# A two-layer graph network on one core: own rows multiplied in their own round, and a finish in four parts

## The chip, the cores and the metric

The kernel runs on one core of a Trainium2 chip. A core has TensorE (matrix products, written PE in a profile, with its weight loads as PEld), VectorE (DVE), ScalarE (ACT), GpSimd (POOL) and SyncE (SP), each working through its own list of instructions, and sixteen DMA engines. The metric is the device time of one execution in microseconds. The kernel before takes 2129.82 us, the median of three runs (2129.74 to 2130.59).

## The reference

Two layers of message passing over 6250 nodes with 512 features, each followed by a residual sum and a layer normalisation. There are 106,250 edges: 50,000 drawn pairs in both directions and one loop for each node, sorted by destination.

```
def _layernorm(x, axis=-1, eps=1e-05):
    m = jnp.mean(x, axis=axis, keepdims=True)
    v = jnp.var(x, axis=axis, keepdims=True)
    return (x - m) / jnp.sqrt(v + eps)
...
    # layer 0: mean over the edges that end in a node
    x_l = x @ W_l.T + b_l
    agg = jax.ops.segment_sum(x_l[src], dst, num_segments=N_NODES)
    deg = jax.ops.segment_sum(jnp.ones_like(src, dtype=x.dtype), dst, num_segments=N_NODES)
    out_l = agg / jnp.maximum(deg, 1.0)[:, None]
    return out_l + x @ W_r.T
...
    # layer 1: mean over the edges that start in a node
    msg = h[dst] @ W_neigh.T + b_neigh
    neigh = jax.ops.segment_sum(msg, src, num_segments=n)
    neigh = neigh / deg[:, None]
    out = jax.nn.relu(h @ W_self.T + b_self + neigh)
    x = h + out
    return (x - mean) * jax.lax.rsqrt(var + LN_EPS) * ln_gamma + ln_beta
...
    x = _layernorm(x + layer0(x), axis=-1)
    x = _layernorm(x + layer1(x), axis=-1)
```

Everything is float32. A mean of products is the product of a mean, so the kernel averages the neighbour rows first and multiplies the average by the weight.

## The kernel before

**Groups, windows, tiles.** `grouped` (L585) does one layer. The sorted edges are cut into four equal columns, and in each of Q rounds the kernel treats one group: up to four windows (one in each column) of 32 nodes, 128 nodes in all. Layer 0 has 60 groups, layer 1 has 66. The last groups have three windows only, because the fourth column ends earlier: 58 and 59 in layer 0, 63 to 65 in layer 1. A tile is 128 edges of each column. A group owns three or four tiles in layer 0 and three in layer 1.

**One round.** The loop at L778 runs over the groups and issues, by hand, the order in which every engine works; nothing reorders it later. In round g:

- `fetch(g + 1)` (L613) lets GpSimd gather the neighbour rows of the next group, one indirect DMA for each tile and window, 128 rows of 2 KB (L609). There are ten buffers `rows` of four windows each.
- `match(g + 1)` (L627) builds 0/1 matrices `hot` on VectorE, `shrink(g + 1)` (L635) sums them for counting.
- `visits(g, ...)` (L691) are the products of `hot` with the rows into `agg`, one visit for each tile, beginning with the last tile of the group before. Four windows of a visit work side by side in TensorE. The visits are issued in three parts: the first two, the third, the rest.
- `count(g)` (L704) multiplies for the numbers of neighbours; VectorE makes the reciprocal from them. `average(g)` (L723) adds the loops in layer 1 (VectorE, L727) and scales `agg` to `mean` (ScalarE, L731).
- `turn(g, v)` (L733, through `transposed`, L571) turns `mean` or the group's own rows `own` by four transposes into the one PSUM buffer `tp`, which ScalarE copies to `meanT` or `ownT`.
- `dense(g, v)` (L737, through `project`, L579) multiplies by a 512 x 512 weight in four products into `po`; `own` starts the sum, `mean` ends it. `po` has one buffer in layer 0 and two in layer 1.
- `close(g)` (L744) starts the generator `finish0` (L530) or `finish1` (L542): bias, residual, statistics (`spread`, L511, with a square root on ScalarE). `store(g)` (L749) runs its rest two rounds after the visits: normalisation, in layer 1 the scale, the shift, the second residual and the second normalisation with a second square root, and then the write to memory, by SP, or, for the three groups named in `ends` (L593), by a scatter of GpSimd.
- `begin(g + 1)` (L675) loads the own rows of the next group, by SP. For two groups near the end of layer 0 (56 and 57) GpSimd gathers them instead (L683), behind the gathers of the same group's neighbours.

So in the round of group g TensorE does: two visits of g; the mean of g-1 turned; the own rows of g-1 multiplied; the third visit; the mean of g-1 multiplied; the own rows of g turned; the remaining visits; the count. In layer 0, steps of sorting the edges for layer 1 are mixed in at the end of each round (`more`, L768) until the sort is done. Layer 1 gathers from `h_d`, which layer 0 writes, so it starts when the last group of layer 0 is stored.

The part of the loop that sets the order around the change:

```
785                    visits(g, slice(0, 2))
786                if g:
787                    turn(g - 1, "mean")
788                    dense(g - 1, "own")
789                if g > 1:
790                    store(g - 2)
...
798                    turn(g, "own")
```

Of the kernel before, what the change touches and what calls it, by code (L numbers as in the profile page):

```python
# [9 lines left out]
F32 = mybir.dt.float32  # L10
# [3 lines left out]
ALU = mybir.AluOpType  # L14
# [4 lines left out]
P = 128  # L19
# [79 lines left out]
def kernel(  # L99
# [16 lines left out]
    nc = tc.nc  # L116
    N, D = x.shape
# [53 lines left out]
    def both(o, a, b, op):  # L171

        nc.vector.scalar_tensor_tensor(o, a, 1.0, b, op0=ALU.mult, op1=op)  # L173
# [347 lines left out]
    def normalize(y, v, mv, root, nr):  # L521

        nc.vector.reciprocal(root[:nr], root[:nr])
        nc.vector.tensor_scalar(y, v, mv[:nr, 0:1], root[:nr], op0=ALU.subtract, op1=ALU.mult)  # L524

    biases = {}

    def finish0(nr, po, own, some, work):  # L530
        po = po[:nr]
        nc.vector.scalar_tensor_tensor(po, biases["bl"][:nr], some[:nr], po,
                                       op0=ALU.mult, op1=ALU.add)
        v = work.tile([P, D], F32, name="v", bufs=1)
        both(v[:nr], po, own[:nr], ALU.add)
        mv, root = spread(v[:nr], nr, work)
        yield
        y = work.tile([P, D], F32, name="y")
        normalize(y[:nr], v[:nr], mv, root, nr)
        yield y  # L540

    def finish1(nr, po, own, some, work):  # L542
        po = po[:nr]
        if some is None:
            both(po, po, biases["bs + bn"][:nr], ALU.add)
        else:
            nc.vector.scalar_tensor_tensor(po, biases["bn"][:nr], some[:nr], po,
                                           op0=ALU.mult, op1=ALU.add)
            both(po, po, biases["bs"][:nr], ALU.add)
        nc.vector.scalar_tensor_tensor(po, po, 0.0, own[:nr], op0=ALU.max, op1=ALU.add)  # L550
        mv, root = spread(po, nr, work)
        yield
        normalize(po, po, mv, root, nr)
        both(po, po, biases["ga"][:nr], ALU.mult)
        both(po, po, biases["be"][:nr], ALU.add)
        y = work.tile([P, D], F32, name="y")
        both(y[:nr], po, own[:nr], ALU.add)
        mv, root = spread(y[:nr], nr, work)
        normalize(y[:nr], y[:nr], mv, root, nr)
        yield y  # L560
# [24 lines left out]
    def grouped(s, table, w_n, w_s, layer, finish, dest, other):  # L585


        with tc.tile_pool(name=f"g{layer}", bufs=2) as work, tc.tile_pool(
# [152 lines left out]
                project(st["po"], st[v + "T"], w_s if v == "own" else w_n, st["nr"],  # L741
                        v == "own", v == "mean")

            def close(g):  # L744
                st = state[g]
                st["finish"] = finish(st["nr"], st["po"], st["own"], st["some"], work)
                next(st["finish"])

            def store(g):  # L749
# [28 lines left out]
            for g in range(Q + 1):  # L778


                if g + 1 < Q:
                    fetch(g + 1)
                    match(g + 1)
                if g < Q:
                    visits(g, slice(0, 2))
                if g:
                    turn(g - 1, "mean")
                    dense(g - 1, "own")
                if g > 1:
                    store(g - 2)  # L790
                if g + 1 < Q:
                    begin(g + 1)
                if g < Q:
                    visits(g, slice(2, 3))
                if g:
                    dense(g - 1, "mean")
                if g < Q:
                    turn(g, "own")
                    visits(g, slice(3, None))
                    count(g)  # L800
                    average(g)
                if g:
                    close(g - 1)
                more(1, True)
                if g + 1 < Q:
                    shrink(g + 1)
                more(5, False)
# [152 lines left out]
```

## Time and profile before

| What | us |
|---|---|
| median of three runs (2129.74 to 2130.59) | 2129.82 |
| the profiled execution | 2130.99 |
| its span, first to last instruction | 2129.2 |
| first gather of layer 0 starts | 30.38 |
| last gather of layer 0 starts | 1086.68 |
| last store of layer 0 is issued | 1106.62 |
| first gather of layer 1 starts | 1111.16 |
| last gather of layer 1 starts | 2095.39 |
| last store of layer 1 is issued | 2123.92 |

The mean granted clock of TensorE in that execution was 0.984 of full speed.

How to read what follows. A line of a group of instructions gives the source line, the engine, the operation, what it writes and reads (with sizes), how many there were, and behind the bar the busy time in microseconds, the mean duration of one in nanoseconds, and the idle time of the engine just before them with what ended it. A line of a timeline gives the start and the duration in microseconds, the engine, the source line and the operation, and in brackets how long the engine was idle before it and what it waited for. One product in float32 is two records, so a multiplication by a weight is "x8" and a visit of three windows is "x6". Records of TensorE overlap a little, so the time of a step is best taken from one start to the next.

### The profile page before, as it was taken

The page shows a single profiled execution, that of the slowest core. Times are in us where ns is not written, and L with a number is a line of the kernel's source. Part 1 is how long each engine was busy: PE and PEld are TensorE (multiplying, and loading weights), DVE is VectorE, ACT ScalarE, POOL GpSimd, SP SyncE. Part 2 cuts the span into 40 slices and gives each one's busy share as a digit, 9 for nine tenths or more (in the row PEclk, how much of TensorE's full clock was granted, in tenths as well). Part 3 has the DMA queues.
Part 4 walks back from the last instruction along what each step waited for, and adds up shares of the span by engine and source line. Part 5 has one row for each costly group of instructions (what it writes and reads, how often), then busy time and mean ns, then how long its engine had stood idle before and what let it go on. Part 6 is the DMA issues. An engine that isn't in the chain of part 4 may idle for free.

```text
span 2129.2 us, 26081 instructions
## 1 busy us (share of the span) xinstructions
PE 1945.1 (91%) x7723; PEld 671.4 (32%) x7723; DVE 1185.0 (56%) x2495; ACT 314.6 (15%) x661; POOL 1554.9 (73%) x1638
## 2 busy tenths in 40 slices
PE   4699999999999998999879999999999999999996
PEld 1132333332323333433222333333333333333332
DVE  2574455564555564342433666666666666666576
ACT  0011111111111111111111111111111111111111
POOL 3777777777777777777747777777777777777773
PEclk9899999999999999999989999999999999999998
DMA  7787877878887878888757888888888888888883
GB/s 225 224 242 235 238 237 237 240 238 240 238 239 237 239 236 240 246 237 242 223 151 227 243 246 246 245 246 244 246 242 249 240 249 241 247 242 246 241 247 109
DMA packets 184527, 499.36 MB, mean 235 GB/s; under 512 B 43946, under 2 KB 46436, under 8 KB 184366
## 3 DMA queue, kind: packets, MB, share of 16 engines
q0 software_dynamic: 130128, 426.11, 67.8%
q1 hardware_dynamic: 51406, 65.89, 9.7%
q10 hardware_dynamic: 2832, 5.51, 0.7%
q8 instruction: 66, 1.08, 0.2%
q14 instruction: 95, 0.78, 0.1%
HBM read 464.74 MB, written 32.96 MB: 234 GB/s over the span
## 4 chain that ended last, share of the span: by engine, by line
DMA 32%; POOL 28%; PE 22%; issue 14%; DVE 3%; POOLq 0%; ACT 0%; SPq 0%; DVEq 0%; ACTq 0%
POOL rows L609 28%; DMA rows<-h_d,idx 17%; DMA rows<-in_x_dram,idx 14%; PE po L582 10%; PE agg L700 9%; PE tp L574 2%; DMA val_i<-in_dst_dram 0%; DVE stats L514 0%; PE turn L465 0%; DVE po L173 0%; DMA own<-in_x_dram,slots 0%; PE deg L709 0%; PE turn L438 0%; PE turn L294 0%; DVE agg L727 0%
## 5 line engine op out<-in xcount | busy, mean ns | idle before, releaser
L700 PE MATMUL agg<-rows,hot 128*32 128x512 f32 x4220 | 900.3, 612 | 134.0 <-DMA rows<-in_x_dram,idx 46.1
L609 POOL DMA_INDIRECT rows<-in_x_dram,idx x834 | 800.7, 960 | 266.4 <-issue 224.7
L609 POOL DMA_INDIRECT rows<-h_d,idx x785 | 744.9, 949 | 242.6 <-issue 200.3
L582 PE MATMUL po<-wa,meanT 128*128 128x512 f32 (+1 forms) x1008 | 466.0, 605 | 0.0
L582 PE MATMUL po<-wb,ownT 128*128 128x512 f32 (+1 forms) x1008 | 456.3, 596 | 0.1
L700 PEld LDWEIGHTS agg<-rows,hot 128*32 128x32 f32 x4220 | 157.0, 109 | 655.0 <-DMA rows<-in_x_dram,idx 242.0
L565 DVE TENSOR_SCALAR inv<-deg 128x1 f32<-128x1 f32 (+1 forms) x60 | 9.5, 158 | 490.4 <-PE deg L709 490.4
L582 PEld LDWEIGHTS po<-wa,meanT 128*128 128x128 f32 (+1 forms) x1008 | 180.2, 188 | 286.7 <-issue 256.5
L582 PEld LDWEIGHTS po<-wb,ownT 128*128 128x128 f32 (+1 forms) x1008 | 181.8, 190 | 183.6 <-issue 183.4
L576 ACT COPY ownT<-tp 128x512 f32<-128x512 f32 (+1 forms) x126 | 73.3, 582 | 800.6 <-PE tp L574 800.6
L718 DVE TENSOR_SCALAR loops<-deg 128x1 f32<-128x1 f32 (+1 forms) x66 | 10.4, 158 | 310.9 <-PE deg L709 302.4
L173 DVE SCALAR_TENSOR_TENSOR srt<-srt 128x448 f32<-128x448 f32 (+3 forms) x313 | 180.4, 617 | 4.0
L731 ACT ACTIVATE mean<-agg,inv 128x512 f32<-128x512 f32 (+1 forms) x126 | 86.6, 687 | 359.3 <-DVE some L568 147.2
L640 DVE TENSOR_REDUCE hotb<-hot 128x128 bf16<-128x512 f32 (+1 forms) x126 | 133.8, 1062 | 0.1
L518 ACT ACTIVATE rstd<-mv,eps 128x1 f32<-128x1 f32 (+1 forms) x192 | 56.5, 294 | 438.9 <-DVE mv L516 435.6
L576 ACT COPY meanT<-tp 128x512 f32<-128x512 f32 (+1 forms) x126 | 73.1, 580 | 193.0 <-PE tp L574 192.9
L173 DVE SCALAR_TENSOR_TENSOR hot<-rel,cols 128x640 f32<-128x640 f32 x126 | 98.1, 778 | 0.2 <-DVE bs L173 0.2
L574 PEld LDWEIGHTS tp<-ident,mean 128*128 128x128 f32 (+1 forms) x504 | 52.8, 141 | 110.7 <-issue 43.5
L574 PE MATMUL tp<-ident,mean 128*128 128x128 f32 (+1 forms) x504 | 82.8, 287 | 4.8 <-ACT mean L731 4.8
L574 PEld LDWEIGHTS tp<-ident,own 128*128 128x128 f32 (+1 forms) x504 | 62.7, 141 | 72.8 <-issue 69.7
L574 PE MATMUL tp<-ident,own 128*128 128x128 f32 (+1 forms) x504 | 75.7, 273 | 5.4 <-DMA own<-in_x_dram,slots 5.4
L524 DVE TENSOR_SCALAR po<-po,mv,rstd 128x512 f32<-128x512 f32 (+1 forms) x66 | 54.0, 818 | 2.4
(151 smaller groups left out, 900.1 us busy)
## 6 DMA issues: line engine op xcount, KB each, us to landing
own<-h_d SPq DMA_DIRECT2D x261, 64.0 KB
out_dram<-y SPq DMA_DIRECT2D x250, 64.0 KB
own<-in_x_dram SPq DMA_DIRECT2D x230, 64.0 KB
h_d<-y SPq DMA_DIRECT2D x227, 64.0 KB
rows<-in_x_dram,idx POOLq DMA_INDIRECT x834
rows<-h_d,idx POOLq DMA_INDIRECT x785
wa<-in_L_gnn_W_l_dram ACTq DMA_DIRECT2D x1, 1024.0 KB
wb<-in_L_gnn_W_r_dram ACTq DMA_DIRECT2D x1, 1024.0 KB
```

Of the source, the lines that this page charges most:

```text
L173: nc.vector.scalar_tensor_tensor(o, a, 1.0, b, op0=ALU.mult, op1=op)
L518: nc.scalar.activation(root[:nr], mv[:nr, 1:2], AF.Sqrt, bias=eps[:nr])
L524: nc.vector.tensor_scalar(y, v, mv[:nr, 0:1], root[:nr], op0=ALU.subtract, op1=ALU.mult)
L565: nc.vector.tensor_scalar(inv[:nr], deg, 1.0, None, op0=ALU.max)
L574: nc.tensor.transpose(p[:, k, :nr], v[:nr, k * P:(k + 1) * P], ident[:nr, :nr])
L576: nc.scalar.copy(t[:, :, :nr], p[:, :, :nr])
L582: nc.tensor.matmul(po[:nr], aT[:, k, :nr], w[:, k, :], start=first and k == 0, stop=end and k == NK - 1)
L609: nc.gpsimd.indirect_dma_start(out=t, out_offset=None, in_=table, in_offset=bass.IndirectOffsetOnAxis(ap=s.idx[:, m:m + 1], axis=0))
L640: nc.vector.tensor_reduce(hb[:, 0, :], hots[g][:, s.X * C:n * C].rearrange("p (v c) h -> p (c h) v", c=C), axis=mybir.AxisListType.X, op=A ...
L700: nc.tensor.matmul(agg[H * c:H * (c + 1), :], hot[:, C * (s.X + v) + c, :], chunks[t][c], start=t == ts[0], stop=t == ts[-1])
L718: nc.vector.tensor_scalar(st["loops"][:nr], deg[:nr, 1:2], 1.0, None, op0=ALU.add)
L731: nc.scalar.mul(st["mean"][:nr], st["agg"][:nr], st["inv"][:nr])
```

## The change

The order of a round becomes: two visits of g; `store(g - 2)` and `begin(g + 1)`; the mean of g-1 turned; the third visit; the own rows of g turned; the mean of g-1 multiplied; the remaining visits; the count; the own rows of g multiplied. In the last round of a layer the own rows of g are turned right behind the mean of g-1, and the third visit and the own product stand between the mean product and the last visit.

The finish is cut into four parts. `ready` (end of the group's own round) does what needs only the own rows: in layer 0 bias times share plus own rows into `v`, in layer 1 own rows plus shift into a new tile `add`. `follow` is called twice in the next round: behind the mean product, for the sums with `po` (and the ReLU), and behind `average`, for the statistics. `store` does the rest. In layer 1 the normalisation, scale, shift and second residual, four operations on VectorE, become two: `(po - mean) * scale` and `that * reciprocal root + add`.

```
     def finish0(nr, po, own, some, work):
-        po = po[:nr]
-        nc.vector.scalar_tensor_tensor(po, biases["bl"][:nr], some[:nr], po,
+        v = work.tile([P, D], F32, name="v")
+        nc.vector.scalar_tensor_tensor(v[:nr], biases["bl"][:nr], some[:nr], own[:nr],
                                        op0=ALU.mult, op1=ALU.add)
-        v = work.tile([P, D], F32, name="v", bufs=1)
-        both(v[:nr], po, own[:nr], ALU.add)
+        yield
+        both(v[:nr], po[:nr], v[:nr], ALU.add)
+        yield
         mv, root = spread(v[:nr], nr, work)
...
     def finish1(nr, po, own, some, work):
         po = po[:nr]
+        add = work.tile([P, D], F32, name="add")
+        both(add[:nr], own[:nr], biases["be"][:nr], ALU.add)
+        yield
...
         nc.vector.scalar_tensor_tensor(po, po, 0.0, own[:nr], op0=ALU.max, op1=ALU.add)
+        yield
         mv, root = spread(po, nr, work)
         yield
-        normalize(po, po, mv, root, nr)
-        both(po, po, biases["ga"][:nr], ALU.mult)
-        both(po, po, biases["be"][:nr], ALU.add)
+        nc.vector.reciprocal(root[:nr], root[:nr])
+        nc.vector.scalar_tensor_tensor(po, po, mv[:nr, 0:1], biases["ga"][:nr],
+                                       op0=ALU.subtract, op1=ALU.mult)
         y = work.tile([P, D], F32, name="y")
-        both(y[:nr], po, own[:nr], ALU.add)
+        nc.vector.scalar_tensor_tensor(y[:nr], po, root[:nr], add[:nr],
+                                       op0=ALU.mult, op1=ALU.add)
         mv, root = spread(y[:nr], nr, work)
...
-            def close(g):
+            def ready(g):
                 st = state[g]
                 st["finish"] = finish(st["nr"], st["po"], st["own"], st["some"], work)
+                next(st["finish"])
+
+            def follow(g):
+                st = state[g]
                 next(st["finish"])
...
                 if g < Q:
                     visits(g, slice(0, 2))
-                if g:
-                    turn(g - 1, "mean")
-                    dense(g - 1, "own")
                 if g > 1:
                     store(g - 2)
                 if g + 1 < Q:
                     begin(g + 1)
+                end = g == Q - 1
+                if g:
+                    turn(g - 1, "mean")
+                if g < Q and not end:
+                    visits(g, slice(2, 3))
                 if g < Q:
-                    visits(g, slice(2, 3))
+                    turn(g, "own")
                 if g:
                     dense(g - 1, "mean")
+                    follow(g - 1)
+                if end:
+                    visits(g, slice(2, 3))
+                    dense(g, "own")
                 if g < Q:
-                    turn(g, "own")
                     visits(g, slice(3, None))
                     count(g)
                     average(g)
                 if g:
-                    close(g - 1)
+                    follow(g - 1)
+                if g < Q:
+                    if not end:
+                        dense(g, "own")
+                    ready(g)
                 more(1, True)
```

## The prediction

> **What bounds the kernel now.** I read the page's groups of instructions, then GpSimd's timeline, then TensorE's at the end of each layer.
>
> ```profile
> PE 1945.1 (91%) x7723; PEld 671.4 (32%) x7723; DVE 1185.0 (56%) x2495; ACT 314.6 (15%) x661; POOL 1554.9 (73%) x1638
> L700 PE MATMUL agg<-rows,hot 128*32 128x512 f32 x4220 | 900.3, 612 | 134.0 <-DMA rows<-in_x_dram,idx 46.1
> L609 POOL DMA_INDIRECT rows<-in_x_dram,idx x834 | 800.7, 960 | 266.4 <-issue 224.7
> L609 POOL DMA_INDIRECT rows<-h_d,idx x785 | 744.9, 949 | 242.6 <-issue 200.3
> ```
>
> TensorE is busier (91% against 73%), yet GpSimd sets the pace. Each of its 1619 gathers takes 0.95 us and the next follows 0.30 us later, whatever they wait for: one in 1.252 us, 1619 x 1.252 = 2027 us of a 2129.2 us span. Beside a few gathers of up to 1.7 us the stream stops only where a layer ends. In layer 1 a round of 12 gathers lasts 12 x 1.252 = 15.0 us; its TensorE work, start to start, is four visits of 0.99, two products of 3.53, two turns of 0.5 and 0.15 for the count, 12.2 us. TensorE's busy time hides waits for single rows. So all that can move the end lies where a layer runs out of gathers. TensorE's timeline at the end of layer 1, then GpSimd's:
>
> ```profile
> 2091.78 0.25 PE L709 MATMUL deg<-ones_b,hotb 128*96 128x1 bf16 x2
> 2091.96 1.92 PE L700 MATMUL agg<-rows,hot 128*32 128x512 f32 x12
> 2094.36 0.55 PE L574 MATMUL tp<-ident,mean 96*128 96x96 f32 x4 [0.48 <-ACT mean L731]
> 2094.74 3.60 PE L582 MATMUL po<-wb,ownT 128*96 128x512 f32 x8
> 2098.27 1.06 PE L700 MATMUL agg<-rows,hot 128*32 128x512 f32 x6
> 2099.26 3.67 PE L582 MATMUL po<-wa,meanT 128*96 128x512 f32 x8
> 2102.77 0.49 PE L574 MATMUL tp<-ident,own 96*128 96x96 f32 x4
> 2103.20 1.06 PE L700 MATMUL agg<-rows,hot 128*32 128x512 f32 x6
> 2104.19 0.25 PE L709 MATMUL deg<-ones_b,hotb 128*96 128x1 bf16 x2
> 2106.55 0.90 PE L574 MATMUL tp<-ident,mean 96*128 96x96 f32 x4 [2.12 <-ACT mean L731]
> 2107.25 4.97 PE L582 MATMUL po<-wb,ownT 128*96 128x512 f32 x8
> 2112.05 3.60 PE L582 MATMUL po<-wa,meanT 128*96 128x512 f32 x8
> ```
> ```profile
> 2095.39 0.95 POOL L609 DMA_INDIRECT rows<-h_d,idx  x1 [0.30 <-issue]
> ```
>
> The last gather starts at 2095.39. Gathers land 3.7 us (1030.39 to 1034.07) to 4.8 us (2051.33 to 2056.16) after their start, so the last rows are there by 2100.2; TensorE visits them at 2103.20. It is late with its own work: in groups 63 to 65 a column of windows is empty, a round has 9 gathers (11.3 us), and TensorE cannot follow. Work moved from behind the last visit to before it is then not hidden.
>
> **The change, part by part.** *Steady rounds:* nothing, in either layer. The cover is the gather stream of 15.0 us a round (12 to 16 gathers, 15 to 20 us, in layer 0) over 12.2 us of TensorE work and the loop of 13.2 us derived below; rows have ten buffers, three rounds' worth. If that cover were gone, each 0.1 us a round over it would cost 6.6 us in 66 rounds. VectorE's saving (0.82 + 0.70 + 0.70 + 0.69 goes, an addition of 0.69 and two fused operations of about 0.75 come: 0.7 us a group) is at nothing there too, and so is layer 0's unchanged count. GpSimd's order stays; SP still stores a group ahead of loading the next own rows, only the load is wanted some 4 us earlier in the next round, and one round is over 11 us.
>
> *End of layer 0.* Two late groups, 56 and 57, fetch their own rows by a GpSimd gather queued behind all their neighbour rows. TensorE now:
>
> ```profile
> 1041.30 3.70 PE L582 MATMUL po<-wa,meanT 128*128 128x512 f32 x8
> 1050.41 1.09 PE L574 MATMUL tp<-ident,own 128*128 128x128 f32 x4 [5.41 <-DMA own<-in_x_dram,slots]
> ```
>
> The wait is covered by the mean product of group 55 ahead of it. The change turns own rows before that product, so the product queues behind the wait, and so do two visits and everything later. From 1050.41 to the last count (1093.60) TensorE takes 43.2 us, about 1.5 of it waits for rows (the two-tile visit at 1080.51 lasts 3.26 to the next start, 1.85 without waits). After: those waits vanish, -1.5; the product of 55, +3.5; the own product of 59, now ahead of the last count, +3.5; the last own turn follows the mean turn at once and waits for the one turning buffer, whose copy starts 0.64 after the turn and lasts 0.48, less the turn's own 0.39, +0.75. Count at 1099.9, 6.3 later. From there to the end of the last product: before 9.2 us (1093.60 to 1102.80); after 1.45 to the turn, 1.15 for turn and copy (no longer under the own product), 3.6: 6.2. Net +3.3. The finish then loses its first operation, 0.79 start to start. **End of layer 0: +2.5 us.** The slow stretch after the long wait (turn 1.09 instead of 0.60) costs the same in both. All of layer 1 shifts with it, since its gathers follow the last store.
>
> *End of layer 1.* The change also moves the store of group g-2, with ScalarE's second square root in it, ahead of the mean turn. ScalarE works in order, so the copy that empties the turning buffer waits for that root, hence for VectorE. Before, the same kind of wait exists, behind the other root, and lies under the own product:
>
> ```profile
> 2083.44 0.29 ACT L518 ACTIVATE rstd<-mv,eps 128x1 f32<-128x1 f32 x1 [1.54 <-DVE mv L516]
> 2083.64 0.28 ACT L645 CAST hotb<-hot 128x128 bf16<-128x128 f32 x1
> 2083.83 0.47 ACT L576 COPY meanT<-tp 128x384 f32<-128x384 f32 x1
> ```
>
> After, queued behind that copy are the own turn (same buffer), the mean product, the last visit, the count. This closes a loop from the end D of one mean product to the next. VectorE, start to start from rows at 2079 to 2089: add biases 0.73, ReLU 0.67, loops and reciprocal 0.50, self loops 0.66, statistics 0.73 and 0.10, the new addition 0.67, reduce 0.93, match 0.73, reciprocal 0.20, two fused operations 2 x 0.75 (not in the trace as such: 0.69 for a scalar-free one, 0.82 for the normalisation from PSUM; I take 0.75, the self-loop row, nearest in form), statistics 0.73 and 0.22; then root 0.20, copy 0.59, own turn 0.53, product 3.53: D + 13.2. TensorE alone gives D + 12.0. In steady rounds rows arrive every 15.0 us and hide both. With 9 gathers the loop decides. Group 62's second tile is gathered by 2056.32; +4.3 landing, 1.04 visit, 0.53 turn, 3.53: D = 2065.7. Then 2078.9, 2092.0 and, the last round having no match (12.4), 2104.4. A visit 0.99, the own product 3.53 and a visit 0.99 put the last count at 2109.9 (2104.19 before). Turn 2.36 later as before, 2112.2. Its copy waits for the root of group 64: from the count 0.28 + 0.50 + 0.66 + 0.83 + 0.67 + 0.20 + 1.50 + 0.95 + 0.20 = 5.8, copy done 2116.1. The mean product then takes 3.6 plus a slow clock. The row for that is 4.97 instead of 3.60 at 2107.25 and 0.90 instead of 0.55 for the turn: 1.6 to 1.7 us in all. End 2121.4, before 2115.65: +5.75. The finish has two fused operations for the four of 0.85, 0.72, 0.73 and 0.73: -1.5. **End of layer 1: +4.2 us.**
>
> The Trainium skill (TensorE: Matmul & The Clock Gate, section "Why this matters for your kernels") says the clock falls only after idle gaps over about 3 us. The trace differs: 2.12 us of idle was enough. By the page the new gap of about 3.3 us stands at its edge; were the clock to stay up, the sum would be 1.6 us less. By the row it falls.
>
> Sum: +2.5 + 4.2 = **+6.7 us**, span 2129.2 to 2135.9. The profiled execution took 2130.99 with that span; the median of the runs is 2129.82. The difference carries over: **2136.5 us**. Bounds: landing 3.7 to 4.8 instead of 4.3, fused operations 0.69 to 0.82 in three rounds, a slow stretch of 0 to 3.6 us (the product wholly at half speed) at the end, 0 to 1.6 at layer 0's end where the gaps of 1.3 and 0.6 us may be enough. Together 2133.5 to 2141.5.
>
> **The rivals.** *Faster, as the order seems to ask:* the own product leaves both tails at no price, -3.5 - 0.8 and -3.5 - 1.5, 2120.5 us. It decides if TensorE waits for the last rows at the end by 3.5 us or more. For: TensorE waits 134 us for rows in all. Against: the last visits (1092.61 and 2103.20) start over 2 us after their rows should have landed (1086.68 + 3.7, 2095.39 + 4.8). 12%.
>
> *No change:* the root does not bind in the last three rounds. With 12.0 a round the D's are 2077.7, 2089.7, 2101.3, count 2106.8, product end 2115.5, finish -1.5, so layer 1 gains 1.6 and layer 0 loses 2.5: 2130.7 us. For: before, TensorE waits for ScalarE only 0.3 to 0.5 us a round. Against: in VectorE's rows the loop is 1.2 us longer. 12%.
>
> *Much slower:* the loop is over 15.0 us in all of layer 1, because an operation of it waits once more: 0.2 us over is 13 us, 2145 to 2150. Against: 1.8 us of room. 8%.
>
> **How the numbers follow.** Forecast 68%. No change and changes within 0.2% (4.3 us) cannot be told apart here. Slower by more, above 2134.1: 0.65 of the forecast and the 0.08: 0.73. Same: 0.12 and the lowest 0.03 of the forecast, 0.15. Faster 0.12. Range 2129.5 to 2142: it takes in the no-change case and leaves out the faster and the much slower one.
>
> **What would show it.** Gathers one in 1.252 us throughout, the last one of layer 0 where it is now; a wait of some 10 us of TensorE for the gathered own rows before the mean product; the last store of layer 0 about 2.5 us later; copies of the mean turn right behind a root in the last rounds of layer 1; over 2 us without TensorE work ahead of the last mean product, and that product longer than 3.6 us. A last count of layer 1 before 2105 (plus the shift) would make it wrong, and so would gaps in the gathers of layer 1.

## The result and the profile after

The changed kernel takes **2160.35 us** (2157.52 to 2161.61, four runs) against 2129.81 us for the kernel before, a ratio of 1.0138 [1.0126, 1.0151]: 30.5 us slower, where 6.7 were forecast. The profiled execution has a span of 2157.4 us (before 2129.2) at a mean granted clock of 0.986. Below, executions are compared by their spans and times by their ratio to the kernel before on the same chip. In some sessions the granted clock was 0.85 to 0.88 for every kernel, the one before included (2533 to 2557 us); gathers don't set the pace there, so from those sessions only what is named as such is used.

From the page of the changed kernel, the rows that the prediction began with (busy time, mean ns of one, and behind the second bar the idle time before them):

```profile
PE 1981.7 (92%) x7723; PEld 659.5 (31%) x7723; DVE 1127.5 (52%) x2429; ACT 310.8 (14%) x661; POOL 1575.6 (73%) x1638
L707 PE MATMUL agg<-rows,hot 128*32 128x512 f32 x4220 | 925.8, 603 | 100.8 <-DMA rows<-in_x_dram,idx 60.7
L616 POOL DMA_INDIRECT rows<-in_x_dram,idx x834 | 808.9, 970 | 266.8 <-issue 223.2
L616 POOL DMA_INDIRECT rows<-h_d,idx x785 | 757.3, 965 | 242.6 <-issue 200.9
```

VectorE has 57.5 us less to do, as the change means it to, and TensorE waits 33 us less for rows. Yet the kernel is slower, and the two gather rows say where: their idle time is what it was (266.8 against 266.4 us, 242.6 against 242.6), but the gathers themselves last 8.2 us longer in layer 0 and 12.4 us longer in layer 1, with the same count. That is 20.6 us of the 28.2 that the span grew.

Cut into stretches by the starts of gathers in GpSimd's timeline, all kernels that ran at a clock of 0.984 to 0.986 (us; labels are those of the experiments):

| Kernel | layer 0, first to last gather | to the first of layer 1 | layer 1, first to last gather | to the end | span |
|---|---|---|---|---|---|
| before | 1056.3 | 24.5 | 984.2 | 33.8 | 2129.2 |
| after | 1064.6 | 27.1 | 996.7 | 37.9 | 2157.4 |
| a_l1_psum | 1065.0 | 28.5 | 985.7 | 37.3 | 2147.4 |
| a_l0_old | 1055.6 | 29.6 | 1001.3 | 37.6 | 2154.6 |
| a_both | 1060.9 | 29.2 | 985.1 | 37.3 | 2143.1 |
| b_add | 1056.4 | 24.6 | 989.6 | 35.1 | 2136.2 |
| c_store_3 | 1058.0 | 28.5 | 985.2 | 32.3 | 2134.9 |
| c_own_4 | 1057.9 | 26.3 | 984.8 | 36.3 | 2136.0 |
| best_4 | 1059.0 | 22.3 | 985.3 | 28.3 | 2125.7 |

The rest of a span, 30.4 to 31.2 us, lies ahead of the first gather. Layer 0's stream varies by some 3 us among kernels with the same finish there (1058 to 1061 in a_both, c_store_3 and c_own_4). After against before, from unrounded starts: +8.3, +2.6, +12.4, +4.1 and, ahead of the first gather, +0.8.

**Which gathers are long.** GpSimd's timeline of the changed kernel in a steady round of layer 1, and VectorE's beside it (start, duration):

```profile
1815.32 0.95 POOL L616 DMA_INDIRECT rows<-h_d,idx  x1 [0.30 <-PE po L589]
1816.58 1.27 POOL L616 DMA_INDIRECT rows<-h_d,idx  x1 [0.30 <-issue]
1818.15 0.94 POOL L616 DMA_INDIRECT rows<-h_d,idx  x1 [0.30 <-issue]
...
1820.65 0.95 POOL L616 DMA_INDIRECT rows<-h_d,idx  x1 [0.30 <-issue]
1821.90 1.20 POOL L616 DMA_INDIRECT rows<-h_d,idx  x1 [0.31 <-issue]
```
```profile
1816.36 0.66 DVE L173 SCALAR_TENSOR_TENSOR add<-own,be 128x512 f32<-128x512 f32 x1
...
1817.90 0.81 DVE L173 SCALAR_TENSOR_TENSOR hot<-rel,cols 128x640 f32<-128x640 f32 x1
...
1821.73 0.55 DVE L524 TENSOR_SCALAR y<-y,mv,rstd 128x512 f32<-128x512 f32 x1
```

The gather at 1816.58 starts under the new addition, which reads `own` and `be`, both in SBUF, and ends at 1817.02: 0.44 us are left, and the gather is 0.32 us longer than 0.95. The one at 1821.90 starts under the second normalisation, SBUF to SBUF, which ends at 1822.28: 0.38 left, 0.25 longer. The one at 1818.15 starts under the match, whose `cols` lies in PSUM, and keeps its 0.94. In layer 1 of this trace 57 of the 59 gathers that start within the addition or the second normalisation keep the same sum to 0.03 us: longer by the rest of that operation less 0.13 us, and by nothing where less is left. None of the 45 gathers that were already running when an addition began was lengthened. Counted over all gathers by the operation under which they start, the later one where two records overlap (lengthened: over 1.05 us):

| Operation of VectorE | inputs | before: starts, lengthened | after |
|---|---|---|---|
| `add<-own,be`, layer 1 | two in SBUF | none | 27, 22 |
| `y<-y,mv,rstd`, layer 1 | one in SBUF, out to SBUF | 26, 7 | 32, 24 |
| `v<-bl_t,some,own`, layer 0 | two in SBUF | none | 34, 14 |
| `y<-po,own` / `y<-po,rstd,add`, layer 1 | one in PSUM, one in SBUF | 50, 0 | 39, 0 |
| `v<-po,own` / `v<-po,v`, layer 0 | one in PSUM, one in SBUF | 26, 0 | 29, 0 |

The rule has an edge: a gather that starts within the first 0.1 us of such an operation often keeps its 0.95 us (both exceptions among the 59 lie there). Leave out these starts and those in an operation's last 0.23 us, where the sum gives under 0.10. In the changed kernel 88 of the 89 starts that remain under operations with two inputs in SBUF (`add`, `v` and the sort's `srt<-srt`) or under a normalisation from SBUF to SBUF are lengthened, but none of 173 under operations with an input in PSUM, and none of 124 under the reduction `hotb<-hot` and the statistics of `v` and `y`, which read one tile in SBUF. So reading from SBUF alone is not enough.

So the theories to be tested are these. **Theory 1:** an operation of VectorE with two inputs in SBUF holds up a gather that starts under it, and the change brings one such operation to each group of each layer in place of operations with an input in PSUM. **Theory 2:** the new order only shifts old operations against the gathers. **Theory 3:** TensorE and VectorE wait for each other in the steady rounds.

### The profile page after: what moved, and what is told of

Same layout as the page of the kernel before. It is cut to its first block, busy times and chain, and to the rows that moved or that the text cites. A ratio compares the mean times of both kernels' runs of the same rounds, so it can differ in the third digit from the quotient of the medians.

```text
span 2157.4 us, 26134 instructions
## 1 busy us (share of the span) xinstructions
PE 1981.7 (92%) x7723; PEld 659.5 (31%) x7723; DVE 1127.5 (52%) x2429; ACT 310.8 (14%) x661; POOL 1575.6 (73%) x1638
## 4 chain that ended last, share of the span: by engine, by line
PE 30%; POOL 27%; DMA 25%; issue 13%; DVE 3%; SPq 0%; ACT 0%; POOLq 0%; DVEq 0%; ACTq 0%
POOL rows L616 27%; PE po L589 16%; DMA rows<-in_x_dram,idx 13%; PE agg L707 11%; DMA rows<-h_d,idx 11%; PE tp L581 2%; DVE stats L514 0%; PE turn L294 0%; PE deg L716 0%; DMA val_i<-in_dst_dram 0%; DMA own<-h_d 0%; DVE hotb L647 0%; DVE y L563 0%; DVE agg L734 0%; DVE hot L173 0%
## 5 line engine op out<-in xcount | busy, mean ns | idle before, releaser
L707 PE MATMUL agg<-rows,hot 128*32 128x512 f32 x4220 | 925.8, 603 | 100.8 <-DMA rows<-in_x_dram,idx 60.7
L616 POOL DMA_INDIRECT rows<-in_x_dram,idx x834 | 808.9, 970 | 266.8 <-issue 223.2
L616 POOL DMA_INDIRECT rows<-h_d,idx x785 | 757.3, 965 | 242.6 <-issue 200.9
L589 PE MATMUL po<-wb,ownT 128*128 128x512 f32 (+1 forms) x1008 | 466.1, 605 | 20.6 <-DVE inv L572 20.6
L589 PE MATMUL po<-wa,meanT 128*128 128x512 f32 (+1 forms) x1008 | 459.2, 599 | 3.8 <-ACT meanT L583 3.8
L173 DVE SCALAR_TENSOR_TENSOR po<-po,bs 128x512 f32<-128x512 f32 (+1 forms) x66 | 46.2, 700 | 349.7 <-PE po L589 349.7
L173 DVE SCALAR_TENSOR_TENSOR v<-po,v 128x512 f32<-128x512 f32 (+1 forms) x60 | 41.4, 689 | 250.6 <-PE po L589 250.5
L581 PE MATMUL tp<-ident,own 128*128 128x128 f32 (+1 forms) x504 | 82.5, 286 | 13.3 <-DMA own<-in_x_dram,slots 9.6
L581 PEld LDWEIGHTS tp<-ident,own 128*128 128x128 f32 (+1 forms) x504 | 52.8, 141 | 117.8 <-issue 104.4
```

The costliest lines, as they stand in the source:

```text
L581: nc.tensor.transpose(p[:, k, :nr], v[:nr, k * P:(k + 1) * P], ident[:nr, :nr])
L589: nc.tensor.matmul(po[:nr], aT[:, k, :nr], w[:, k, :], start=first and k == 0, stop=end and k == NK - 1)
L616: nc.gpsimd.indirect_dma_start(out=t, out_offset=None, in_=table, in_offset=bass.IndirectOffsetOnAxis(ap=s.idx[:, m:m + 1], axis=0))
L707: nc.tensor.matmul(agg[H * c:H * (c + 1), :], hot[:, C * (s.X + v) + c, :], chunks[t][c], start=t == ts[0], stop=t == ts[-1])
```

## The experiments on the cause

**The addition of layer 1 with its shift in PSUM.** `be_p` is a copy of the shift, made once.

```
+                biases["be_p"] = ps.tile([P, D], F32, name="be_p")
+                nc.vector.tensor_copy(biases["be_p"], biases["be"])
...
-        both(add[:nr], own[:nr], biases["be"][:nr], ALU.add)
+        both(add[:nr], own[:nr], biases.get("be_p", biases["be"])[:nr], ALU.add)
```

> The changed kernel, but in layer 1 the new addition own + shift reads the shift from a copy in PSUM instead of from SBUF; same operations, same order. Theory 1 (a VectorE operation with both inputs in SBUF makes a gather that starts during it wait): the 21 long gathers that start in that addition (7.4 us) go, and most of the 23 in the second normalisation, which follow them, fall back to the 7 of the kernel before: layer 1's gathers take 985 to 990 us instead of 996.7, the time is 2148 to 2153. Theory 2 (the new order moves VectorE's old operations against the gathers, the place of an operand does not matter): no change, 2157 to 2162. Theory 3 (TensorE's and VectorE's loop paces the rounds of layer 1): no change either.

Measured: 2146.09 us (two executions, 2143.05 and 2149.14), ratio 1.0072 [1.0051, 1.0092], 2 us below the expected range; layer 1's stream 985.7 us, back by 11 us with every instruction in its place. GpSimd's and then VectorE's timeline of this kernel:

```profile
1767.01 0.95 POOL L618 DMA_INDIRECT rows<-h_d,idx  x1 [0.30 <-issue]
```
```profile
1766.83 0.65 DVE L173 SCALAR_TENSOR_TENSOR add<-own,be_p 128x512 f32<-128x512 f32 x1
```

The gather starts 0.18 us into the addition, with 0.47 us left, and keeps its 0.95. Of 43 gathers that start under the addition none is longer; 38 of them have more than 0.23 us left.

**Layer 0's sum in its old form,** bias and own rows added to `po` behind the product, the rest of the change kept.

```
+        yield
...
-        nc.vector.scalar_tensor_tensor(v[:nr], biases["bl"][:nr], some[:nr], own[:nr],
+        nc.vector.scalar_tensor_tensor(po[:nr], biases["bl"][:nr], some[:nr], po[:nr],
                                        op0=ALU.mult, op1=ALU.add)
-        yield
-        both(v[:nr], po[:nr], v[:nr], ALU.add)
+        both(v[:nr], po[:nr], own[:nr], ALU.add)
```

> The changed kernel, but layer 0's finish again works on po, as before the change: bias times share plus po, then plus own rows, both after the mean product, so that each has an input in PSUM. Theory 1: the 17 long gathers in v go (4.8 us) and some of the sorting ones with them; layer 0's gathers take 1057 to 1061 us instead of 1064.6; the last store of layer 0 loses 0.8 us of the finish again; time 2152 to 2157. Theory 2: 2158 to 2163.

Measured: 2156.44 us, 1.012 [1.010, 1.0141]; layer 0's stream 1055.6 us, as before (1057 to 1061 expected). Layer 1's is 1001.3, 4.6 us longer than in the changed kernel with the same code: 35 gathers start under its additions and 31 are lengthened. How many starts meet such an operation differs from execution to execution.

**Both.**

> Both edits together. Theory 1: both layers' gather streams are within some 3 us of the kernel before; what is left is the price of the order at the two ends, 2.6 + 4.0 us, and the 0.8 us of finish at layer 0's end: 2136 to 2145. Theory 2: 2157 to 2163.

Measured: 2140.95 us, 1.0040 [1.0026, 1.0054]. The page of this kernel:

```profile
L618 POOL DMA_INDIRECT rows<-in_x_dram,idx x834 | 805.2, 965 | 266.6 <-issue 218.5
L618 POOL DMA_INDIRECT rows<-h_d,idx x785 | 745.7, 950 | 242.7 <-issue 196.3
```

Layer 1's gathers are at 745.7 us, 0.8 from the kernel before. The new order and the four parts of the finish are all still there, so neither theory 2 nor theory 3 has anything left to explain in layer 1. Layer 0's stream, 1060.9 us, stays 4.6 us over the kernel before, more than the expected 3; its gathers last 4.5 us longer, mostly under the sort.

**The addition alone, in the kernel before.** Its result is used by nothing.

```
+                if g < Q and s.loops:
+                    extra = work.tile([P, D], F32, name="extra")
+                    nr = state[g]["nr"]
+                    both(extra[:nr], state[g]["own"][:nr], biases["be"][:nr], ALU.add)
```

> The kernel before, plus in layer 1 the addition own + shift for each group after the statistics of the group before, both inputs in SBUF, its result unused; the order on TensorE is the old one. Theory 1: gathers that start in it are long, by 0.3 us each, some 20 of 66 rounds if the phase is as in the changed kernel, and more or fewer if not; layer 1's gathers take 4 to 14 us more: 2134 to 2144. Theory 2: the new order is missing, so nothing happens: 2129 to 2131. Theory 3: the same as theory 2.

Measured: 2136.57 us, 1.0021 [1.0010, 1.0033]; layer 1's stream 989.6 us. GpSimd's and then VectorE's timeline of that kernel:

```profile
1230.35 1.28 POOL L609 DMA_INDIRECT rows<-h_d,idx  x1 [0.30 <-issue]
```
```profile
1230.15 0.66 DVE L173 SCALAR_TENSOR_TENSOR extra<-own,be 128x512 f32<-128x512 f32 x1
```

The gather starts 0.20 us into the addition, and 0.46 less 0.13 is the 0.33 that it lasts longer. Of the 29 that start under it 20 are lengthened.

**The same addition with the shift in PSUM.** The diff is the one above with `be_p`.

> The kernel before with one unused addition a group in layer 1, as in the run that had the shift in SBUF, but with the shift in PSUM: the same operation, the same place, the same 0.69 us of VectorE, one of its two inputs elsewhere. Theory 1 (an operation of VectorE with two inputs in SBUF holds up a gather that starts under it): the added operation lengthens no gather, layer 1's stream of gathers is 984 to 986 us as in the kernel before (989.6 with the shift in SBUF), time 2129 to 2132. Rival (any further operation of VectorE shifts or slows the stream): as with the shift in SBUF, 2134 to 2139.

> The kernel before with the unused addition in layer 1 and the shift in PSUM, once more, since the granted clock was 0.87 in that session for every kernel, the one before too (2556.62 us), and gathers then don't set the pace. At a clock near 0.985: theory 1 (two SBUF inputs hold up gathers) layer 1's stream 984 to 986 us, time 2129 to 2132; rival (any further VectorE operation costs it) 989 to 990 us, 2134 to 2139.

> The kernel before with the unused addition in layer 1, its shift in PSUM; with the shift in SBUF it was 1.0021 [1.0010, 1.0033] and layer 1's stream 989.6 us. At a clock near 0.985: theory 1 (two SBUF inputs hold up gathers) stream 984 to 986 us, ratio 0.999 to 1.001; rival (any further VectorE operation costs it) 989 to 990 us, ratio 1.002 to 1.003.

Measured: 1.0002 [0.9992, 1.0011] of the kernel before, at a clock of 0.87, and 1.0005 [0.9991, 1.0019] and 1.0001 [0.9989, 1.0013] in two more sessions at that clock. Gathers don't set the pace there: layer 1's stream lasts 1171 to 1183 us, with 742.3 to 744.9 us of gathers in it (744.9 in the kernel before). So the streams of 984 or 989 us that were expected were not put to the test, and the times say little; the gathers say more:

```profile
1561.10 0.94 POOL L611 DMA_INDIRECT rows<-h_d,idx  x1 [0.30 <-issue]
```
```profile
1560.90 0.66 DVE L173 SCALAR_TENSOR_TENSOR extra<-own,be_p 128x512 f32<-128x512 f32 x1
```

The same addition, the same 0.20 us into it, and the gather lasts 0.94. In the three profiled executions 42, 44 and 50 gathers start under it, and none is lengthened; but most of them start in its last 0.13 us, where the sum above gives nothing in either case, and only 9, 9 and 5 have more than 0.23 us left. The weight therefore lies on the kernels at 0.985 to 0.986: in a_l1_psum, a_both, c_store_3 and c_own_4 together 144 gathers start with more than 0.23 us left of the addition with `be_p`, and none is lengthened; with `be`, in the changed kernel, a_l0_old and b_add, it is 73 of 77. For the addition theory 1 is shown: the operand's place decides, with operation, order and duration unchanged. It does not cover the second normalisation, which reads one tile and lengthens gathers in either kernel; no run moves its operand.

## The experiments on the two ends

Each of these kernels ran in three or four sessions, and gathers set the pace only in the last of them. With the operands moved (a_both) the kernel is still slower than before. The prediction has two terms for that, each with one edit against it; both edits start from a_both.

**The store behind the turn of the mean:** ScalarE's second square root no longer stands ahead of the copy.

```
-                if g > 1:
-                    store(g - 2)
-                if g + 1 < Q:
-                    begin(g + 1)
                 end = g == Q - 1
                 if g:
                     turn(g - 1, "mean")
+                if g > 1:
+                    store(g - 2)
+                if g + 1 < Q:
+                    begin(g + 1)
```

> The changed kernel with both of its SBUF operands gone (2140.95 us), and the store of group g-2 and the load of the next own rows put behind the turn of the mean, so that the copy of that turn no longer waits for ScalarE's second square root. Prediction's step for the end of layer 1: the tail from the last gather to the end, 37.3 us there, falls to 32 to 34.5 us, no idle time of 3.2 us ahead of the last mean product; layer 0's end stays (29.2 us from its last gather to the first of layer 1). Time 2136 to 2138.5. Rival (the tail is longer because the own product stands ahead of the last visit, not because of the root): tail 36.5 or more, time 2140 to 2142.

> Both SBUF operands gone (2140.95 us at a clock of 0.985), store of group g-2 behind the turn of the mean; once more for the same reason. Prediction's step for layer 1's end: tail from the last gather 37.3 to 32 to 34.5 us, no 3.2 us of idle ahead of the last mean product, time 2136 to 2138.5. Rival (own product ahead of the last visit is what costs): tail 36.5 or more, 2140 to 2142.

> Both SBUF operands gone (2140.95 us at a clock of 0.985), store of group g-2 behind the turn of the mean. Seen so far at 0.86: the copy of the last mean turn comes 0.62 us of idle after the turn instead of 3.2. Prediction's step for layer 1's end, at 0.985: tail from the last gather 37.3 to 32 to 34.5 us, time 2136 to 2138.5. Rival (own product ahead of the last visit is what costs): tail 36.5 or more, 2140 to 2142. At 0.87 for all kernels: 1.003 to 1.005 of the kernel before, as twice before.

Measured at 0.986: 2136.58 us, 1.0013 [1.0004, 1.0023], and the tail is 32.3 us against 37.3. (At 0.86 to 0.87, twice: 1.0050 and 1.0032.) TensorE's timeline of this kernel at the end:

```profile
2104.22 3.60 PE L589 MATMUL po<-wa,meanT 128*96 128x512 f32 x8
...
2115.70 0.55 PE L581 MATMUL tp<-ident,mean 96*128 96x96 f32 x4 [2.12 <-ACT mean L740]
2116.87 5.37 PE L589 MATMUL po<-wa,meanT 128*96 128x512 f32 x8 [0.62 <-ACT meanT L583]
```

The wait for the copy is 0.62 us; in a_both it was 3.19. The mean products of the rounds before, the last of them in the first row, start 12.00, 11.95 and 11.56 us apart, which is TensorE's own work. The own product still stands ahead of the last visit, so that rival is out.

**The own turn behind the mean product.**

```
-                if g < Q:
-                    turn(g, "own")
                 if g:
                     dense(g - 1, "mean")
                     follow(g - 1)
+                if g < Q:
+                    turn(g, "own")
```

> The changed kernel with both of its SBUF operands gone (2140.95 us), and the own rows turned behind the mean product of the group before instead of ahead of it, so that no mean product queues behind the wait for the gathered own rows. Prediction's step for the end of layer 0: the mean product of group 55 (3.5 us) goes under the wait again, and the time from the last gather of layer 0 to the first of layer 1 falls from 29.2 to about 25.7 us (24.5 in the kernel before); layer 1's tail falls by 0 to 2 us, the wait of 0.9 to 1.1 us of the own turn for the turning buffer in each of the last rounds being gone. Time 2135.5 to 2138. Rival (that wait costs nothing because TensorE catches up before the last visit): 28.5 to 29.5 us there, time 2139.5 to 2142.

> Both SBUF operands gone (2140.95 us at a clock of 0.985), own rows turned behind the mean product; once more for the same reason. Prediction's step for layer 0's end: 29.2 to about 25.7 us from its last gather to layer 1's first, time 2135.5 to 2138. Rival (the wait for own rows costs nothing): 28.5 to 29.5 us, 2139.5 to 2142. New from the session at 0.87, where this edit cost 3% against its neighbour: if the same edit also binds a steady round at full clock, layer 1's stream of gathers, 985.1 us, would grow by over 10 us and the time with it.

> Both SBUF operands gone (2140.95 us at a clock of 0.985), own rows turned behind the mean product. Prediction's step for layer 0's end: 29.2 to about 25.7 us from its last gather to layer 1's first, time 2135.5 to 2138. Rival (the wait for own rows costs nothing): 28.5 to 29.5 us, 2139.5 to 2142. Second rival, from two sessions at 0.85: the mean product then has only one visit to cover its copy and binds steady rounds: layer 1's stream, 985.1 us, over 995.

> Both SBUF operands gone (2140.95 us at a clock of 0.985), own rows turned behind the mean product. Prediction's step for layer 0's end: 29.2 to about 25.7 us from its last gather to layer 1's first, time 2135.5 to 2138. Rival (the wait for own rows costs nothing): 28.5 to 29.5 us, 2139.5 to 2142. Second rival, from the sessions at 0.85: steady rounds bind too, layer 1's stream, 985.1 us, over 995.

Measured at 0.986: 2139.67 us beside 2134.63, 1.0020 [1.0011, 1.0030]. The time lies over the expected 2138 and in the rival's range, because the kernel before takes 4.8 us more in that session than in the first; the ratio fits the expectation. From layer 0's last gather to layer 1's first it is 26.3 us against 29.2 (25.7 expected, 28.5 to 29.5 by the rival), and layer 1's stream is 984.8 us, so neither rival holds at this clock. TensorE's timeline of this kernel:

```profile
1042.09 3.70 PE L589 MATMUL po<-wa,meanT 128*128 128x512 f32 x8
1051.91 1.08 PE L581 MATMUL tp<-ident,own 128*128 128x128 f32 x4 [6.12 <-DMA own<-in_x_dram,slots]
```

The mean product lies under the wait for the gathered own rows again. From the last gather to the last count it is 9.9 us against 14.5 in a_both, a gain of 4.6; 1.7 of it is lost again because the last product takes 5.37 us here and 3.67 there. In three sessions at 0.85 to 0.87 this kernel took 3.2 to 3.7% more than the kernel before, where the kernel with the store moved, in two of them, took 0.3 to 0.5% more. In one of these executions TensorE waited 276.5 us ahead of the mean products, 184.5 of it for `meanT`. But with the store moved it waited 171.1 us for the same copy ahead of the own turns, and a_both did not run in these sessions, so why this order is so dear there stays open. An order that costs little while gathers set the pace can be dear where they don't.

**Only the ends treated anew,** from the kernel before. In the last round of a layer part of the own product stands between the last count and the turn of the mean, the rest under the copy of that turn; the fused finish stands only where no gathers are left.

```
+                    if end:
+                        dense(g, "own", range(NK - 2 + layer))
                     average(g)
...
-                    dense(g - 1, "own")
+                    dense(g - 1, "own", range(NK - 2 + layer if g == Q else 0, NK))
...
+                st["finish"] = finish(st["nr"], st["po"], st["own"], st["some"], work,
+                                      g >= Q - 1 - layer)
```

> The kernel before in all steady rounds; only the last group of each layer is treated anew. Its own product is cut: three (layer 1) or two (layer 0) of its four steps stand between the last count and the turn of the mean, the rest under the copy of that turn. The fused finish stands only where no gathers are left: last two groups of layer 1, last group of layer 0. Theory 1 with the prediction's rows: layer 1's end, 11.5 us from the last count to the end of the last product, becomes 7.7 (-3.8), its finish -1.5; layer 0's end 9.2 becomes 7.6 (-1.6), its finish -0.8; streams of gathers as before (1056 and 984 us). Time 2121 to 2125. Rival (the finish of group Q-2 on VectorE or the wait for the mean then binds): 2125 to 2129.

> The kernel before in steady rounds, the two ends treated anew; once more for the same reason (it was 0.9965 [0.9953, 0.9976] of the kernel before at 0.87). At a clock near 0.985: 2121 to 2125 us, streams 1056 and 984 us, layer 1's end 11.5 to 7.7 us from last count to end of last product, layer 0's 9.2 to 7.6. Rival (finish of group Q-2 or the wait for the mean binds): 2125 to 2129.

> The kernel before in steady rounds, the two ends treated anew by the prediction's rows. At a clock near 0.985: 2121 to 2125 us, streams of gathers 1056 and 984 us, layer 1's end 11.5 to 7.7 us from last count to end of last product, layer 0's 9.2 to 7.6. Rival (finish of group Q-2 or the wait for the mean binds): 2125 to 2129. Where the clock is again 0.87 for all kernels, it is 0.995 to 0.997 of the kernel before, as in two sessions so far.

> The kernel before in steady rounds, the two ends treated anew by the prediction's rows. Seen at 0.875: 7.5 us from the last count to the end of the last product in layer 1 and 7.8 in layer 0 (7.7 and 7.6 expected). At 0.985: 2121 to 2125 us, streams of gathers 1056 and 984 us; at 0.87 for all kernels 0.996 to 0.998 of the kernel before.

Measured at 0.986: 2128.58 us beside 2134.51, **0.9973 [0.9963, 0.9982]**, so it beats both kernels; at 0.87 to 0.88, in three sessions, 0.9958 to 0.9974. The time is over the expected 2121 to 2125: that session's kernel before stands 4.7 us higher, and in the profiled execution the two streams are 2.7 and 1.1 us longer than in the kernel before, where nothing was expected. The two ends are 2.2 and 5.5 us shorter than before, where 2.4 and 5.3 were expected. TensorE's timeline at the end:

```profile
2105.51 0.25 PE L726 MATMUL deg<-ones_b,hotb 128*96 128x1 bf16 x2
2105.62 2.79 PE L599 MATMUL po<-wb,ownT 128*96 128x512 f32 x6
2108.25 0.49 PE L591 MATMUL tp<-ident,mean 96*128 96x96 f32 x4
2108.59 1.02 PE L599 MATMUL po<-wb,ownT 128*96 128x512 f32 x2
2109.45 3.60 PE L599 MATMUL po<-wa,meanT 128*96 128x512 f32 x8
```

No wait is left in these rows, the granted clock over them is 1.00, and the last product keeps its 3.60 us: from the count to its end 7.5 us, 11.5 before.

## Why the prediction was wrong, and where it was right

**"Steady rounds: nothing" failed.** The prediction took the gather stream for a fixed cover, 1.252 us a gather whatever the other engines do, and asked only whether TensorE's work and VectorE's loop fit under it. They do: the gathers' idle time did not change, and the fourth case, a loop over 15.0 us, did not come, although the time lies above even its 2145 to 2150. What failed is the fixed 1.252 us: the stream itself depends on VectorE's operands. The term was put at 0 and is +20.7 us (8.3 and 12.4). In layer 1 it is the new addition and the second normalisation. In layer 0, 4.8 us of the 8.3 stand under the new sum `v`; most of the rest stands under the sort's `srt<-srt`, which have both inputs in SBUF in either kernel (130 starts, 28 lengthened by over 0.10 us before, 141 and 39 after; most of the others start in the first 0.05 us of the operation). The change does not touch the sort; how many of its operations meet a start differs among executions (27 in a_l0_old, 35 in a_both). The VectorE saving was counted by durations and not by what is read from where: in layer 1, operations that read `po` went, and one that reads two tiles in SBUF came. "Gaps in the gathers of layer 1" were named as what would make it wrong; it was not gaps but longer gathers. The sign "the last one of layer 0 where it is now" failed too: it starts 9.1 us later.

The row that speaks of it was in the trace of before. The prediction passes over "a few gathers of up to 1.7 us". The longest lasts 1.41 us, and 1.7 is about its distance to the next start; 35 in layer 0 and eight in layer 1 are over 1.05 us, and seven of these eight start under `y<-y,mv,rstd`. An estimate could have been made from it: an operation of 0.66 us lengthens starts in its first 0.53 us, one start comes every 1.252 us, so 42% of 66 groups are hit by 0.265 us on average, 7.4 us. Measured under the addition in the changed kernel: 7.7 us. The second normalisation went from 1.5 to 5.5 us in the same execution, and to 0.9 in a_both; by the same estimate with its mean of 0.61 us it would be some 6 us at random, so the kernel before was below chance. Why its starts miss the gathers there, and meet them in the changed kernel, is not settled. Both fell together when the addition's operand was moved; but in b_add, with the old order, the addition lengthens 20 gathers and the second normalisation only five (1.0 us), so long gathers alone do not bring it about.

The Trainium skill (SBUF — State Buffer, section "Who interferes with whom") says that VectorE and GpSimd share a pair of ports under an exclusive lock, that an operation with at most one input in SBUF stays off it outside two-port modes, which `tensor_scalar`, the form of the second normalisation, can enter, and that one with two contends with a GpSimd instruction that reads SBUF, because its second input comes through the shared read interface. That agrees with none lengthened in 43 starts with the shift in PSUM and 22 in 27 without. The same section infers that a `tensor_tensor` does not stall the generation of DMA descriptors; for these gathers, which read their indices `idx`, and the `scalar_tensor_tensor` here, 22 in 27 say otherwise, and the measurement decides. That the lock is what makes them wait is the page's account; the runs show the waiting, its length and the operand that causes it.

**"End of layer 0: +2.5" was right in sum, 2.6, by two terms that were both off; that is luck.** From the last gather to the last count it is +4.7 us where 6.3 were predicted: gathers end 9.1 us later, so TensorE is less late. From the count to the end of the product it is -1.3 where -3.0 was predicted, because the last product ran slow after 1.24 and 0.62 us of idle (granted clock 0.70 during it). TensorE's timeline of the changed kernel:

```profile
1058.86 1.08 PE L581 MATMUL tp<-ident,own 128*128 128x128 f32 x4 [9.59 <-DMA own<-in_x_dram,slots]
1059.74 4.73 PE L589 MATMUL po<-wa,meanT 128*128 128x512 f32 x8
...
1107.38 0.20 PE L716 MATMUL deg<-ones_b,hotb 128*96 128x1 bf16 x1
1108.83 0.55 PE L581 MATMUL tp<-ident,mean 96*128 96x96 f32 x4 [1.24 <-ACT mean L738]
1110.00 5.26 PE L589 MATMUL po<-wa,meanT 128*96 128x512 f32 x8 [0.62 <-ACT meanT L583]
```

The wait of "some 10 us for own rows before the mean product" is there, with the product behind it; c_own_4 shows what that costs, 2.9 us of the end, or 4.6 up to the last count. Where the stream ends as before (a_l0_old) the last store of layer 0 is issued 4.5 us later, against 3.3 by the prediction without the finish. The difference, 1.2 us, is about what two waits for VectorE take, 0.57 and 0.67 us, which the changed kernel doesn't have. With one `po` in layer 0 and the sum in its old form behind the product, the own product waits for the finish of the group before; the second row names the sum `v`, the first a later operation. In a_l0_old's timeline:

```profile
1071.35 3.67 PE L589 MATMUL po<-wb,ownT 128*128 128x512 f32 x8 [0.57 <-DVE inv L572]
...
1096.48 3.64 PE L589 MATMUL po<-wb,ownT 128*96 128x512 f32 x8 [0.67 <-DVE v L173]
```

**"End of layer 1: +4.2" was right in mechanism and in sum, 4.1, but the sum again by terms that offset each other.** It is +3.7 from the last gather to the last count (5.7 predicted, and 4.2 in a_both, whose stream in layer 1 is as long as before), +1.2 to the end of the last product (none predicted), -1.6 to the last store (-1.5 predicted) and +0.7 behind it. TensorE's and then ScalarE's timeline of the changed kernel:

```profile
2097.93 3.62 PE L589 MATMUL po<-wa,meanT 128*128 128x512 f32 x8
...
2110.83 3.60 PE L589 MATMUL po<-wa,meanT 128*96 128x512 f32 x8
...
2122.97 3.60 PE L589 MATMUL po<-wa,meanT 128*96 128x512 f32 x8
...
2132.08 0.25 PE L716 MATMUL deg<-ones_b,hotb 128*96 128x1 bf16 x2
2134.45 0.55 PE L581 MATMUL tp<-ident,mean 96*128 96x96 f32 x4 [2.12 <-ACT mean L738]
2138.20 6.56 PE L589 MATMUL po<-wa,meanT 128*96 128x512 f32 x8 [3.20 <-ACT meanT L583]
```
```profile
2137.49 0.29 ACT L518 ACTIVATE rstd<-mv,eps 96x1 f32<-96x1 f32 x1 [2.73 <-DVE mv L516]
2137.69 0.46 ACT L583 COPY meanT<-tp 128x384 f32<-128x384 f32 x1
```

The loop through ScalarE's root sets the last rounds: mean products 12.90 and 12.14 us apart, predicted 13.2 and 12.4. The copy stands right behind the root, 3.20 us of idle ahead of the last product (about 3.3 predicted), and the product lasts 6.56 instead of 3.60 at a granted clock of 0.56: 3.0 us more, where the row taken for the slow clock gave 1.6 to 1.7. c_store_3 shows the root to be the cause. It also shows the slow clock without a gap of 3 us: its last product lasts 5.37 us at a granted clock of 0.68, behind gaps of 2.12 and 0.62, so the rule of about 3 us that the prediction weighed (the Trainium skill, TensorE: Matmul & The Clock Gate, section "Why this matters for your kernels") doesn't hold here.

**The rivals.** The own product does leave both tails, but not by moving it ahead of the last visits, where TensorE is late: best_4 gets most of what the first rival hoped for (7.7 of 9.3 us at the two ends) by filling waits behind the last count instead.

## What to carry to other kernels

Where GpSimd issues a stream of gathers that sets the pace, go through VectorE's operations by where their inputs lie, not only by duration: here one with two inputs in SBUF cost a tenth of a microsecond a group on average, one of the same duration with an input in PSUM cost nothing. A stream whose idle time is unchanged can still be slower, so compare the mean of one gather (949 ns against 965 in layer 1) before looking for gaps. Work goes best into a wait that exists (behind the last count), not ahead of a visit for which its engine is already late.

## What the runs showed of the hardware

A gather of GpSimd that starts under an operation of VectorE with two inputs in SBUF, or under the normalisation from SBUF to SBUF, lasts longer by the rest of that operation less 0.13 us, under the addition of 0.66 us up to 0.52 us more on 0.95; starts in the operation's first 0.1 us often escape, and a gather already running when the operation starts lasts no longer (0 of 45 and 0 of 49 under the additions), and the operation itself keeps its 0.66 us. The same idle time of TensorE has different prices: after 1.24 and 0.62 us a product of 3.60 us took 3.67 us in a_l0_old, at a granted clock of 1.00, and 5.26 in the changed kernel, at 0.70. What decides between the two is open.
